# The last graph layer's dense products in 32-column tiles of TensorE, issued three rows at a time

## The chip, the cores and the metric

One Trainium2 chip, one of its cores. The metric is the device time of one execution in microseconds (us); runs are given by their median. The engines are TensorE (PE; its weight loads are listed apart as PEld), VectorE (DVE), ScalarE (ACT), GpSimd (POOL) and SyncE (SP), which here issues DMAs. All data of the changed part are fp32, but for the table of edge counts, which is bf16.

## The reference

A network of four layers on a graph of 3125 nodes with 256 features and 100,000 edges. Each layer adds a graph convolution and a mixer to x, then a feed-forward part with experts. The change is in the last layer's graph convolution, an attention over edges with four heads of 64 columns:

```python
xn = _layernorm(x)
x = x + _L3_gnn_ref(xn, edge_index, W, att_src, att_dst) + _L3_mix_ref(xn[None], ...)[0]
x = x + _L3_ffn_ref(_layernorm(x)[None], ...)[0]

def _gat_conv(x, edge_index, W, att_src, att_dst):
    xp = (x @ W).reshape(n, N_HEADS, HEAD_DIM)
    e = leaky_relu(a_src[src] + a_dst[dst], 0.2)
    e_exp = exp(e - segment_max(e, dst)[dst])
    alpha = e_exp / segment_sum(e_exp, dst)[dst]
    out = segment_sum(alpha[:, :, None] * xp[src], dst)
```

The mixer of this layer is a linear attention with a two-layer network behind it; the feed-forward part sends each node to one of eight experts.

## The kernel before, in words

Nodes lie in 25 blocks of 125 (`NB`, `P`); targets are also cut into pieces of 500 (`PIECES`, `PW`), the seventh of 125. The kernel computes this layer's sums over edges densely. For every source block, head and range of targets it forms a matrix z (source x target) of weights: the exponential of the leaky sum splits into factors of source and target, which ACT (L1965) and DVE (L1968) combine with the number of edges between each source and target, read from `ctt_d` into `cs`. The target factors lie in `rows`, a part of `xn`, loaded anew for each pair of pieces by `target_rows`. PE then multiplies z by the source block's features `xr` (L1971). `xr` has 65 columns per head: 64 features and a column of ones, whose product is the sum of the weights.

`l3_dense` takes the pieces two at a time, which gives three groups of 1000 targets and one of 125. For each group of 1000 it makes two passes of two heads each; the last group is one pass of four heads. A pass runs over the 25 source blocks (a row is one source block in one pass) and accumulates in four PSUM banks, one for each head and piece. So a row has two z of 125 x 1000 and four products of 65 x 500. At the end of a pass the banks are copied to SBUF (`evac`, turn by turn on DVE and ACT, L163 and L165), each block of 125 targets is turned on PE (L1987, in the last pass L1996), and `finish` (L1925 to L1932) divides by the sum, clips at zero and adds to `x`.

Next to `l3_dense` runs the mixer (`l3_mix_by_pieces`), a generator as it is; `together` (L1905) takes steps from the one that is behind, at a pace of 1.0 to 1.15. When both have delivered a piece (`arrive`), `follow` in `l3_ffn` normalizes it, turns it, finds its gate and expert (L2204 to L2255) and sends its rows to the experts by indirect DMAs on POOL; `l3_dense` hands its pieces over after row 5 of the next pass. After that the experts run. A scheduler that works at build time orders the instructions of each engine by their priorities, which go by the order in the program, and by its own estimates; each engine runs its list in order.

Of the kernel before, what the change touches and what calls it, by code (L numbers as in the profile page):

```python
# [12 lines left out]
F32 = mybir.dt.float32  # L13
# [4 lines left out]
AF = mybir.ActivationFunctionType  # L18
OP = mybir.AluOpType
# [4 lines left out]
N = 3125  # L24
D = 256
P = 125
NB = 25
# [10 lines left out]
PW = 500  # L38
# [52 lines left out]
def _tables():  # L91
# [12 lines left out]
    t[NT1 * 128:NT1 * 128 + NB, 0] = np.arange(NB) * P  # L104
    return np.ascontiguousarray(t.reshape(NT1 + 1, 128, 4).transpose(1, 2, 0))
EARLY = 0.25
PIECES = [(i, min(PW, N - i)) for i in range(0, N, PW)]


class Net:  # L110
    NE, TS = 16, 384

    def __init__(self, tc, a, ctx):
# [30 lines left out]
        self.col = col  # L144
        self.mean = c.tile([128, HB, len(PIECES)], F32, name="mean_p")

# [65 lines left out]
    def norm(self, src, dst):  # L212

        for i, w in PIECES:
            b0, b1 = i // P, (i + w) // P
            self.norm_rows(b1 - b0, src[:, b0:b1], dst[:, b0:b1])

    def expect(self, parts, follow=None, lag=0):

        self.waiting = {i: parts for i, _ in PIECES}  # L220
        self.follow = follow or self.norm_turn_piece
# [25 lines left out]
    def turn(self, src, dst):  # L247
        for i, w in PIECES:
            self.turn_piece(src, dst, i, w)
# [34 lines left out]

    def times_rows(self, pool, g, rows, e, out, add, pieces=PIECES):

# [107 lines left out]
    def counts(self, sb, wk, pt, px, py):  # L394
# [3 lines left out]
        self.cnt_d = self.dram.tile([NB, P, N], BF, name="cnt_d")  # L398
        self.ctt_d = self.dram.tile([len(PIECES), P, NB, PW], BF, name="ctt_d")
        i4 = sb.tile([128, 150, 4], BF, name="i4")  # L400
# [649 lines left out]
    def l0_ffn(self, fast=False):  # L1050
# [4 lines left out]
        with ExitStack() as s:  # L1055
# [69 lines left out]
            with ExitStack() as s2:  # L1125
                sums = None
                if fast:
# [3 lines left out]
                    with tc.issue_after(placed.ins):  # L1131
                        for part in sums:
                            if part > EARLY:
                                break
# [7 lines left out]
                for i in range(NT):  # L1142
# [29 lines left out]
                    for part in sums or ():  # L1172
                        if i + 1 < NT and part > EARLY + (1 - EARLY) * (i + 1) / NT:
                            break
# [662 lines left out]
    def l3_gnn_mix(self, before, arrivals):  # L1837
# [5 lines left out]
        nc, a = self.nc, self.a  # L1843
        with ExitStack() as s:
            ms = s.enter_context(self.pool("m3_sb"))
            with self.pool("m3_w") as sb:
                w = self.load_w(sb, "L3_gnn_W")
# [6 lines left out]
            sb = s.enter_context(self.pool("g3_sb"))  # L1854
            wk = s.enter_context(self.pool("g3_wk", 2))
            pa = s.enter_context(self.pool("g3_ps", 1, space=PSUM))
            xr = sb.tile([P, NB, 4, 65], F32, name="xr")
            nc.gpsimd.memset(xr[:, :, :, 64:65], 1.0)
            al = sb.tile([P, NB, 8], F32, name="al")
            for b in range(NB):  # L1860
                ps = self.bank()
                self.mm_tok(ps[:P, :264], self.xt, b, wx)
                nc.vector.tensor_copy(xr[:, b, :, :64], ps[:P, :D].rearrange("p (h d) -> p h d", h=4))
                nc.scalar.copy(al[:, b, :], ps[:P, 256:264])
            m = sb.tile([P, 8], F32, name="m")
            nc.vector.tensor_reduce(m, al.rearrange("p b h -> p h b"), axis=AX.X, op=OP.max)
            ps = self.bank()
# [5 lines left out]
            ps = self.bank()  # L1873
# [4 lines left out]
            bias = sb.tile([P, 4], F32, name="bias3")  # L1878
# [8 lines left out]
            r = sb.tile([P, 4, NB], F32, name="r3")  # L1887
            for h in range(4):
                nc.scalar.activation(r[:, h], al[:, :, 4 + h], AF.Exp, bias=bias[:, h:h + 1], scale=0.8)
            ps = self.bank()  # L1890
# [6 lines left out]
            us = sb.tile([P, 3, NB, 4], F32, name="us")  # L1897
# [16 lines left out]

    def l3_dense(self, sb, wk, pa, xr, us, r_d):

        nc = self.nc
        few = sb.tile([P, NB, 4], F32, name="few")
        free = self.xn.rearrange("p b d -> p (b d)")
        rows = free[:, :8 * PW].rearrange("p (h d) -> p h d", h=4)  # L1920
        at = free[:65, 8 * PW:12 * PW].rearrange("p (h d) -> p h d", h=2)

        def finish(b, h0, nh, acc):

            nc.vector.tensor_scalar(few[:, b, h0:h0 + nh], acc[:, :, 64], 1e-20, None, op0=OP.is_lt)  # L1925
            rd = wk.tile([P, 4], F32, name="rd")
            nc.vector.tensor_scalar(rd[:, :nh], acc[:, :, 64], 1e-20, None, op0=OP.max)
            nc.vector.reciprocal(rd[:, :nh], rd[:, :nh])
            t = wk.tile([P, 4, 64], F32, name="tf")
            nc.vector.tensor_mul(t[:, :nh], acc[:, :, :64], rd[:, :nh, None].to_broadcast([P, nh, 64]))  # L1930
            v = self.x[:, b, h0 * 64:(h0 + nh) * 64]
            nc.vector.scalar_tensor_tensor(v, t[:, :nh].rearrange("p h d -> p (h d)"), 0.0, v,  # L1932
                                           op0=OP.max, op1=OP.add)

        def target_rows(i, h0):

            n = min(2 * PW, N - i)
            for h in (h0, h0 + 1):
                if n > 0:
                    self.move(nc.sync, rows[:P, h, :n], r_d[h, i:i + n].partition_broadcast(P))  # L1940

        done, there = 0, []
        for h0 in (0, 2):
            target_rows(0, h0)
        for p0 in range(0, len(PIECES), 2):
            pcs = PIECES[p0:p0 + 2]
            n = sum(w for _, w in pcs)
            hg = 4 if n < PW else 2
            for h0 in range(0, 4, hg):
                acc = {}  # L1950
                for h in range(hg):
                    for k in range(len(pcs)):
                        acc[h, k] = pa.tile([65, 512], F32, name=f"acc{h * len(pcs) + k}")
                for b in range(NB):
                    cs = wk.tile([P, 2, PW], BF, name="cs", bufs=3)
                    if len(pcs) == 2:
                        self.move(nc.sync, cs, self.ctt_d[p0:p0 + 2, :, b, :].rearrange("k p d -> p k d"))
                        c = cs.rearrange("p k d -> p (k d)")
                    else:
                        self.move(nc.sync, cs[:, 0, :n], self.ctt_d[p0, :, b, :n])  # L1960
                        c = cs[:, 0, :n]
                    for h in range(hg):
                        k4 = h0 + h
                        t = wk.tile([P, 2 * PW], F32, name="t5")
                        nc.scalar.activation(t[:, :n], rows[:, k4, :n], AF.Relu, bias=us[:, 2, b, k4:k4 + 1],  # L1965
                                             scale=us[:, 0, b, k4:k4 + 1])
                        z = wk.tile([P, 2 * PW], F32, name="z", bufs=3)
                        nc.vector.scalar_tensor_tensor(z[:, :n], t[:, :n], us[:, 1, b, k4:k4 + 1], c,  # L1968
                                                       op0=OP.add, op1=OP.mult)
                        for k, (i, w) in enumerate(pcs):  # L1970
                            nc.tensor.matmul(acc[h, k][:, :w], xr[:, b, k4, :], z[:, k * PW:k * PW + w],  # L1971
                                             start=(b == 0), stop=(b == NB - 1))
                        done += n
                    yield done / (NB * N * 4)
                    if b == 5:
                        for i in there:
                            self.arrive(i)
                        there = []
                if hg == 2:
                    target_rows(pcs[0][0] + 2 * PW, h0)  # L1980
                    for h in range(2):
                        for k, (i, w) in enumerate(pcs):
                            self.evac(at[:, h, k * PW:k * PW + w], acc[h, k][:, :w])
                    for j in range(n // P):
                        ps = self.bank()
                        for h in range(2):
                            nc.tensor.transpose(ps[:P, h * 65:(h + 1) * 65], at[:, h, j * P:(j + 1) * P],  # L1987
                                                self.ident[:65, :65])
                        finish(p0 * 4 + j, h0, 2, ps[:P, :130].rearrange("p (h c) -> p h c", h=2))
                        yield done / (NB * N * 4)  # L1990
                else:
                    for h in range(4):
                        self.evac(at[:, h // 2, h % 2 * P:(h % 2 + 1) * P], acc[h, 0][:, :P])
                    ps = self.bank()
                    for h in range(4):
                        nc.tensor.transpose(ps[:P, h * 65:(h + 1) * 65], at[:, h // 2, h % 2 * P:(h % 2 + 1) * P],  # L1996
                                            self.ident[:65, :65])
                    finish(p0 * 4, 0, 4, ps[:P, :260].rearrange("p (h c) -> p h c", h=4))

            there = [i for i, w in pcs]  # L2000
        for i in there:
            self.arrive(i)
        nc.vector.tensor_reduce(self.viol[:P, 5:6], few.rearrange("p b h -> p (b h)"), axis=AX.X, op=OP.add)
# [421 lines left out]
```

## Time and profile before

| | us |
|---|---|
| median of 11 runs | 4812.44 (4802.48 to 4816.42) |
| the profiled execution | 4803.38 |
| its span | 4801.5 |
| PE busy in the span | 3740.6 |
| DVE busy | 2512.8 |
| ACT busy | 1303.2 |
| POOL busy | 1023.3 |
| mean clock granted to PE | 0.856 |

The profile is of one execution. A group's line gives line, engine, operation, output and inputs, shape and count; then busy time in us, the mean length of one in ns, and the engine's idle time ahead of it with what ended most of it. Lengths of PE's records contain a modelled end, so the distance between starts is the better measure of pace. An fp32 product shows as two records.

### The profile page before, as it was taken

How to read it: one execution, taken by the hardware profiler on the slowest of the kernel's cores; microseconds unless marked ns; L12 is line 12 of the kernel's file. 1: busy time of each engine (PE TensorE's matmuls, PEld its weight loads, DVE VectorE, ACT ScalarE, POOL GpSimd, SP SyncE). 2: the span in 40 equal slices, each digit the busy share in tenths (PEclk: the TensorE clock that was granted, in tenths of full speed). 3: DMA queues.
4: the chain of work that ended last, by engine and by line, in shares of the span. 5: the costliest groups of instructions: out<-in, count | busy, mean ns of one | idle time of the engine just before them, and what ended most of it. 6: DMA issues, size and time to landing. Idle time of an engine off the chain costs nothing. (4 is left out here: it accounts for less than half of the span.)

```text
span 4801.5 us, 50401 instructions
## 1 busy us (share of the span) xinstructions
PE 3740.6 (78%) x16695; PEld 2500.3 (52%) x16695; DVE 2512.8 (52%) x8604; ACT 1303.2 (27%) x2336; POOL 1023.3 (21%) x1041
## 2 busy tenths in 40 slices
PE   1887896599657899998454656666598999999698
PEld 0676795377534565555343445545365444444466
DVE  5877326544566319964222223333346677677544
ACT  1466100022123232233000000000145655556521
POOL 2000002300243000002666666666000000000011
PEclk8686896699878799999666777878799999999699
DMA  6244611344330000002333333333301222122232
GB/s 183 60 115 130 145 48 36 90 136 137 96 80 18 25 14 7 14 7 60 92 90 93 93 90 92 92 89 94 126 1 49 57 61 68 50 54 54 58 121 66
DMA packets 256035, 358.86 MB, mean 75 GB/s; under 512 B 62719, under 2 KB 199350, under 8 KB 255765
## 3 DMA queue, kind: packets, MB, share of 16 engines
q1 hardware_dynamic: 135900, 176.07, 12.5%
q0 software_dynamic: 62832, 126.93, 9.9%
q10 hardware_dynamic: 57033, 52.54, 3.9%
q8 instruction: 136, 2.23, 0.2%
q14 instruction: 134, 1.10, 0.1%
HBM read 268.73 MB, written 94.97 MB: 76 GB/s over the span
## 5 line engine op out<-in xcount | busy, mean ns | idle before, releaser
L1617 PE MATMUL acc<-hg,to 128*125 128x256 f32 x2042 | 597.7, 448 | 314.7 <-issue 160.6
L1601 POOL DMA_INDIRECT hg<-hx_d,idx x782 | 745.2, 953 | 414.9 <-issue 212.4
L1617 PEld LDWEIGHTS acc<-hg,to 128*125 128x125 f32 x2042 | 443.3, 224 | 447.5 <-issue 195.9
L1971 PE MATMUL acc<-z,xr 125*65 125x500 f32 (+1 forms) x1400 | 574.7, 553 | 15.0 <-DVE z L1968 13.5
L1612 DVE TENSOR_SCALAR to<-iota_w,rel_b,kw 128x125 f32<-128x125 f32 (+1 forms) x782 | 250.1, 376 | 428.2 <-remote 281.2
L1965 ACT ACTIVATE t<-xn,us 125x1000 f32<-125x1000 f32 (+1 forms) x400 | 409.4, 1037 | 237.5 <-DVE z L1968 226.0
L1968 DVE SCALAR_TENSOR_TENSOR z<-t,us,cs 125x1000 f32<-125x1000 f32 (+1 forms) x400 | 409.5, 1028 | 115.2 <-PE acc L1971 94.3
L1971 PEld LDWEIGHTS acc<-z,xr 125*65 125x65 f32 x1400 | 187.8, 144 | 314.6 <-issue 268.2
L261 PE MATMUL ps<-xt,w 128*128 128x500 f32 (+1 forms) x672 | 268.3, 546 | 1.6 <-DMA w<-in_L_ffn_W_dram 1.6
L1536 DVE SCALAR_TENSOR_TENSOR junk<-iota_w,rel_b,lock 128x125 f32<-128x125 f32 (+1 forms) x782 | 249.4, 401 | 0.0
L797 ACT ACTIVATE k<-k 125x128 f32<-125x128 f32 x50 | 15.8, 316 | 781.8 <-DVE k L796 495.6
L2255 POOL DMA_INDIRECT bx_d<-row,slot x25 | 31.2, 1249 | 886.5 <-ACT t L1965 420.9
L589 PE MATMUL ps<-y,cb 125*125 125x256 bf16 x1875 | 215.2, 280 | 0.0
L589 PEld LDWEIGHTS <-cb 125*125 125x125 bf16 x1875 | 214.0, 141 | 0.1
L190 ACT ACTIVATE rstd_t<-rstd_t 125x4 f32<-125x4 f32 (+2 forms) x86 | 17.2, 203 | 685.6 <-DVE rstd_t L189 561.2
L255 PE MATMUL ps<-wo,h 128*125 128x256 f32 x800 | 187.7, 386 | 3.6 <-ACT h L1439 2.6
L1445 DVE SCALAR_TENSOR_TENSOR x<-ps,lg,x 125x256 f32<-125x256 f32 x200 | 94.1, 489 | 173.5 <-PE ps L255 173.5
L261 PEld LDWEIGHTS ps<-xt,w 128*128 128x128 f32 x672 | 122.5, 193 | 114.0 <-issue 101.9
L261 PE MATMUL ps<-h,w 128*128 128x500 f32 (+1 forms) x448 | 179.5, 541 | 2.3 <-ACT h L1434 1.6
L255 PEld LDWEIGHTS ps<-wo,h 128*125 128x125 f32 x800 | 142.7, 187 | 66.0 <-ACT h L1439 43.7
L470 PE MATMUL t<-ky,lo 128*128 128x75 bf16 (+4 forms) x1251 | 138.9, 253 | 39.5 <-ACT ct L473 25.1
L243 PE MATMUL ps<-ident,xn 125*128 125x125 f32 x300 | 57.7, 342 | 139.9 <-DVE xn L209 128.9
(566 smaller groups left out, 6244.4 us busy)
## 6 DMA issues: line engine op xcount, KB each, us to landing
cs<-ctt_d SPq DMA_DIRECT2D x150, 218.8 KB
w<-in_L_ffn_w_dram SPq DMA_DIRECT2D x52, 512.0 KB
cnt_d<-cd SPq DMA_DIRECT2D x25, 683.6 KB
cb<-cnt_d SPq DMA_DIRECT2D x25, 683.6 KB
ctt_d<-ct ACTq DMA_DIRECT2D x6, 2734.4 KB
hg<-hx_d,idx POOLq DMA_INDIRECT x782
b0x_d<-zero SPq DMA_DIRECT2D x1, 9984.0 KB
xb<-b0x_d SPq DMA_DIRECT2D x26, 384.0 KB
```

Source lines behind the costliest of these rows:

```text
L255: self.nc.tensor.matmul(ps, xt[:, h, b * P:(b + 1) * P], w[:, h, :], start=(h == 0), stop=(h == k - 1))
L261: self.nc.tensor.matmul(ps, w[:, h, :], xt[:, h, i:i + n], start=(h == 0), stop=(h == k - 1))
L470: nc.tensor.matmul(t[:, w * 25 * r:(w + 1) * 25 * r], lo[:, :, n % 4], ky[:, :25 * r, n % 4], start=(j == 0), stop=(j == ws[w0 + w][2] - 1))
L589: nc.tensor.matmul(ps[:P, :D], cf[k][:, h * P:(h + 1) * P], y3[:, b0 + k, j, :], start=(k == 0 and j == 0), stop=(k == m - 1 and j == 2))
L1445: nc.vector.scalar_tensor_tensor(self.x[:, b, :], ps[:P, :D], g[:, b, e:e + 1], self.x[:, b, :], op0=OP.mult, op1=OP.add)
L1536: nc.vector.scalar_tensor_tensor(junk[:, :m * P], self.iota_w[:, :m * P], rel[:, c:c + 1], lock[:, b:b + m].rearrange("p b n -> p (b n)"), ...
L1601: nc.gpsimd.indirect_dma_start(out=hg[:, j, :], out_offset=None, in_=hx, in_offset=bass.IndirectOffsetOnAxis(ap=idx[:, c0 + j:c0 + j + 1], ...
L1612: nc.vector.tensor_scalar(to, self.iota_w[:, :nb * P], rel[:, c:c + 1], kw[:, j:j + 1], op0=OP.is_equal, op1=OP.mult)
L1617: nc.tensor.matmul(acc[k], to[:, (k - b) * P:(k - b + 1) * P], hg[:, j, :D], start=(c == first[k]), stop=(c == last[k]))
L1965: nc.scalar.activation(t[:, :n], rows[:, k4, :n], AF.Relu, bias=us[:, 2, b, k4:k4 + 1], scale=us[:, 0, b, k4:k4 + 1])
L1968: nc.vector.scalar_tensor_tensor(z[:, :n], t[:, :n], us[:, 1, b, k4:k4 + 1], c, op0=OP.add, op1=OP.mult)
L1971: nc.tensor.matmul(acc[h, k][:, :w], xr[:, b, k4, :], z[:, k * PW:k * PW + w], start=(b == 0), stop=(b == NB - 1))
```

## The change

`xr` loses its column of ones. A row's products are now 12 (four banks become three): for each piece, two heads by two halves of 32 columns fill the four 32-column tiles of one bank, and a third bank takes, for each piece and head, the product of z with 32 columns of ones, which gives the sum 32 times over. z has four buffers in place of three, and t moves to two spare pieces of `xn`. Dependencies without a semaphore chain all tile products of a row and its z's, so that they keep their order on PE; they are recorded at a higher priority (600). Every third row (`BURST`) the last product that isn't one of them is noted, and the burst that begins three bursts later (`LAG`) stands behind it. A pass's banks are three out of four in turn. At the end of a pass all targets of a piece are turned by whole transposes of 128 columns, and the division is done for a piece at a time.

The order of the built program on PE, from the first to the last of these products: before, 700 products of L1971 and 731 others, in 313 stretches; after, 2100 tile products and 700 others, in 153 stretches.

```diff
+BURST, LAG = 3, 3
...
-            xr = sb.tile([P, NB, 4, 65], F32, name="xr")
-            nc.gpsimd.memset(xr[:, :, :, 64:65], 1.0)
+            xr = sb.tile([P, NB, 4, 64], F32, name="xr")
...
+        spare = [free[:P, j * PW:(j + 2) * PW] for j in (8, 10)]
+        groups = [PIECES[p:p + 2] for p in range(0, len(PIECES), 2)]
...
+        def finish(b, nb, h0, nh, acc):
+
+            w, nu = nb * P, len(acc) - 1
+            at = wk.tile([128, 3, PW], F32, name="at", bufs=1)
+            for k in range(nu + 1):
+                self.evac(at[:, k, :w], acc[k][:, :w])
+            ps = self.bank()
+            for j in range(nb):
+                nc.tensor.transpose(ps[:P, j * 128:(j + 1) * 128], at[:, nu, j * P:(j + 1) * P], self.ident)
+            sums = ps[:P, :nb * 128].rearrange("p (j q r) -> p j q r", j=nb, r=32)[:, :, :, 0]
...
+            for k in range(nu):
...
+                for j in range(nb):
+                    nc.tensor.transpose(ps[:P, j * 128:(j + 1) * 128], at[:, k, j * P:(j + 1) * P], self.ident)
+                t = wk.tile([P, 4, 2, 64], F32, name="tf")
+                nc.vector.tensor_mul(t[:, :nb], ps[:P, :nb * 128].rearrange("p (j h d) -> p j h d", j=nb, d=64),
+                                     rd[:, :nb, 2 * k:2 * k + 2, None].to_broadcast([P, nb, 2, 64]))
...
+                units = [(h0, k, w) for h0 in hs for k, (_, w) in enumerate(pcs)]
+                acc = [pa.tile([128, 512], F32, name=f"acc{(turn + j) % 4}") for j in range(3)]
+                turn += 3
...
-                        t = wk.tile([P, 2 * PW], F32, name="t5")
+                        t = spare[h % 2]
...
-                        z = wk.tile([P, 2 * PW], F32, name="z", bufs=3)
+                        z = zs[h] = wk.tile([P, 2 * PW], F32, name="z", bufs=4)
...
-                            nc.tensor.matmul(acc[h, k][:, :w], xr[:, b, k4, :], z[:, k * PW:k * PW + w],
-                                             start=(b == 0), stop=(b == NB - 1))
+                    if steps % BURST == 0:
+                        marks.append(next((i for i in reversed(nc.cur_bb.bb.instructions)
+                                           if i.engine == mybir.EngineType.PE and i.name not in own), None))
+                        if len(marks) > LAG and marks[-1 - LAG] is not None:
+                            made.append(marks[-1 - LAG])
+                    steps += 1
+                    with self.tc.high_priority(600):
+                        for out, left, h0, j, k, w, q in (
+                                [(acc[u], xr[:, b, h0 + j, f:f + 32], h0, j, k, w, 64 * j + f)
+                                 for u, (h0, k, w) in enumerate(units) for j in range(2) for f in (0, 32)]
+                                + [(acc[2], self.ones[:P, :32], h0, j, k, w, 64 * u + 32 * j)
+                                   for u, (h0, k, w) in enumerate(units) for j in range(2)]):
+                            mm = nc.tensor.matmul(out[q:q + 32, :w], left, zs[h0 + j][:, k * PW:k * PW + w],
+                                                  start=(b == 0), stop=(b == NB - 1), tile_position=(0, q))
+                            for i in made:
+                                self.tc.add_manual_dep(mm.ins, i.name, row, reason="in one row")
+                            made = [mm.ins]
+                            own.add(mm.ins.name)
```

More of the change, by code (lines that the diff above doesn't have):

```diff
@@ L1862, in l3_gnn_mix @@
                 self.mm_tok(ps[:P, :264], self.xt, b, wx)
-                nc.vector.tensor_copy(xr[:, b, :, :64], ps[:P, :D].rearrange("p (h d) -> p h d", h=4))
+                nc.vector.tensor_copy(xr[:, b], ps[:P, :D].rearrange("p (h d) -> p h d", h=4))
                 nc.scalar.copy(al[:, b, :], ps[:P, 256:264])
@@ L1920, in l3_dense @@
         rows = free[:, :8 * PW].rearrange("p (h d) -> p h d", h=4)
[L1921 to L1939, printed above, removed]
-                    self.move(nc.sync, rows[:P, h, :n], r_d[h, i:i + n].partition_broadcast(P))
-        done, there = 0, []
+        spare = [free[:P, j * PW:(j + 2) * PW] for j in (8, 10)]
+        groups = [PIECES[p:p + 2] for p in range(0, len(PIECES), 2)]
+        def target_rows(g, h0):
+            if g < len(groups):
+                i, n = groups[g][0][0], sum(w for _, w in groups[g])
+                for h in (h0, h0 + 1):
+                    self.move(nc.sync, rows[:P, h, :n], r_d[h, i:i + n].partition_broadcast(P))
@@ new lines, in finish @@
+        def finish(b, nb, h0, nh, acc):
[7 more added lines that the diff above has]
+            sums = ps[:P, :nb * 128].rearrange("p (j q r) -> p j q r", j=nb, r=32)[:, :, :, 0]
+            rd = wk.tile([P, 4, 4], F32, name="rd")
+            f = wk.tile([P, 4, 4], F32, name="fw")
+            nc.vector.tensor_scalar(f[:, :nb], sums, 1e-20, None, op0=OP.is_lt)
+            nc.vector.tensor_scalar(rd[:, :nb], sums, 1e-20, None, op0=OP.max)
+            nc.vector.reciprocal(rd[:, :nb], rd[:, :nb])
+            for k in range(nu):
+                bk, hk = (b + 4 * k, h0) if nh == 2 else (b, 2 * k)
+                nc.vector.tensor_copy(few[:, bk:bk + nb, hk:hk + 2], f[:, :nb, 2 * k:2 * k + 2])
+                ps = self.bank()
+                for j in range(nb):
[3 more added lines that the diff above has]
+                                     rd[:, :nb, 2 * k:2 * k + 2, None].to_broadcast([P, nb, 2, 64]))
+                v = self.x[:, bk:bk + nb, hk * 64:hk * 64 + 128]
+                nc.vector.scalar_tensor_tensor(v, t[:, :nb].rearrange("p j h d -> p j (h d)"), 0.0, v,
+                                               op0=OP.max, op1=OP.add)
@@ L1943, in l3_dense @@
+        done, there, turn, made, marks, steps, own = 0, [], 0, [], [], 0, set()
+        row = mybir.DependencyInfo(mybir.DependencyClass.NoSync, mybir.DependencyReason.DATA)
         for h0 in (0, 2):
             target_rows(0, h0)
-        for p0 in range(0, len(PIECES), 2):
-            pcs = PIECES[p0:p0 + 2]
+        for g, pcs in enumerate(groups):
+            b0 = pcs[0][0] // P
             n = sum(w for _, w in pcs)
[L1948 to L1953, printed above, removed]
+            for hs in ((0, 2),) if len(pcs) == 1 else ((0,), (2,)):
+                units = [(h0, k, w) for h0 in hs for k, (_, w) in enumerate(pcs)]
+                acc = [pa.tile([128, 512], F32, name=f"acc{(turn + j) % 4}") for j in range(3)]
+                turn += 3
@@ L1956, in l3_dense @@
                     if len(pcs) == 2:
-                        self.move(nc.sync, cs, self.ctt_d[p0:p0 + 2, :, b, :].rearrange("k p d -> p k d"))
+                        self.move(nc.sync, cs, self.ctt_d[2 * g:2 * g + 2, :, b, :].rearrange("k p d -> p k d"))
                         c = cs.rearrange("p k d -> p (k d)")
                     else:
-                        self.move(nc.sync, cs[:, 0, :n], self.ctt_d[p0, :, b, :n])
+                        self.move(nc.sync, cs[:, 0, :n], self.ctt_d[2 * g, :, b, :n])
@@ L1961, in l3_dense @@
                         c = cs[:, 0, :n]
-                    for h in range(hg):
-                        k4 = h0 + h
-                        t = wk.tile([P, 2 * PW], F32, name="t5")
-                        nc.scalar.activation(t[:, :n], rows[:, k4, :n], AF.Relu, bias=us[:, 2, b, k4:k4 + 1],
-                                             scale=us[:, 0, b, k4:k4 + 1])
-                        z = wk.tile([P, 2 * PW], F32, name="z", bufs=3)
[L1968 to L1971, printed above, removed]
-                                             start=(b == 0), stop=(b == NB - 1))
-                        done += n
+                    zs, made = {}, made[-1:]
@@ new lines, in l3_dense @@
+                    for h in [h0 + j for h0 in hs for j in range(2)]:
+                        t = spare[h % 2]
+                        nc.scalar.activation(t[:, :n], rows[:P, h, :n], AF.Relu, bias=us[:, 2, b, h:h + 1],
+                                             scale=us[:, 0, b, h:h + 1])
+                        z = zs[h] = wk.tile([P, 2 * PW], F32, name="z", bufs=4)
+                        made.append(nc.vector.scalar_tensor_tensor(z[:, :n], t[:, :n], us[:, 1, b, h:h + 1], c,
+                                                                   op0=OP.add, op1=OP.mult).ins)
@@ L1974, in l3_dense @@
+                    done += n * 2 * len(hs)
                     yield done / (NB * N * 4)
@@ L1978, in l3_dense @@
                         there = []
[L1979 to L1998, printed above, removed]
+                for h0 in hs:
+                    target_rows(g + 1, h0)
+                finish(b0, pcs[0][1] // P, hs[0], 2 * len(hs), acc)
+                yield done / (NB * N * 4)
             there = [i for i, w in pcs]
```

## The prediction

> **What bounds the kernel now.** I read the page first (busy shares, the 40 slices, the costliest groups), then the window of the changed lines by engine, then the waits inside it, then the order of TensorE's products there. The last graph layer's products are line L1971; its first and last starts bound a window from 3672 to 4532 us, 860 of the span's 4801.5 us.
>
> ```profile
> L1971 PE MATMUL acc<-z,xr 125*65 125x500 f32 (+1 forms) x1400 | 574.7, 553 | 15.0 <-DVE z L1968 13.5
> L1965 ACT ACTIVATE t<-xn,us 125x1000 f32<-125x1000 f32 (+1 forms) x400 | 409.4, 1037 | 237.5 <-DVE z L1968 226.0
> L1968 DVE SCALAR_TENSOR_TENSOR z<-t,us,cs 125x1000 f32<-125x1000 f32 (+1 forms) x400 | 409.5, 1028 | 115.2 <-PE acc L1971 94.3
> ```
> ```profile
> 3672.00:4532.00 860.00, 828.75 (x2620) 379.88 (x2618) 598.51 (x1293) 512.72 (x627) 30.04 (x24) 0.97 0.20 54
> 4444.00:4532.00 88.00, 69.27 (x303) 43.65 (x301) 59.48 (x245) 58.39 (x121) 9.55 (x8) 0.73 0.11 25
> ```
>
> The second fence is the busy time by engine of the window and of its last 88 us: PE, weight loads, DVE, ACT, POOL, then the granted clock. PE is busy 829 of 860 us; DVE 599, ACT 513. DVE sits idle 94 us in front of L1968 because PE has not yet released a z; PE waited for a z only 13.5 us. So PE bounds the window, and 575 of its 829 us are L1971. The other 254 us are the mixer and the routing, which run in between. Only the last 88 us are different: there a row has four heads of 125 targets, ACT needs 4 x 0.49 us a row, PE is busy 69 of 88 us.
>
> The products in between are long chains across engines, and today they cost PE no idle time. The timeline of PE inside one of the mixer's attention steps:
>
> ```profile
> 4319.49 1.84 PE L1971 MATMUL acc<-z,xr 125*65 125x500 f32 x4
> 4321.17 0.27 PE L1340 MATMUL ps<-ident,o 125*128 125x125 f32 x1
> 4321.28 2.68 PE L1971 MATMUL acc<-z,xr 125*65 125x500 f32 x6
> 4323.79 0.48 PE L1340 MATMUL ps<-ident,o 125*128 125x125 f32 x3
> 4324.11 3.52 PE L1971 MATMUL acc<-z,xr 125*65 125x500 f32 x8
> 4327.46 0.38 PE L1340 MATMUL ps<-ident,o 125*128 125x125 f32 x2
> ```
>
> Columns: start, length, line, number of records. Each L1340 transpose waits for four DVE steps on its block, and L1971 fills every wait. This also gives the pace: from 4321.28, six records later, to 4323.79, and from 4324.11, eight records later, to 4327.46, 0.419 us each. One fp32 product of 500 columns is two such records (1400 records for 700 products), 0.838 us.
>
> **The change, part by part.**
>
> *The products.* A row (one source block, two heads, 1000 targets) has 4 products of 65 columns now: 4 x 0.838 = 3.35 us. After, it has 12 products of 32 columns, in three rounds over the four column tiles. If the four tiles of a round stream side by side, a round costs one product's time: 3 x 0.838 = 2.51 us. The saving is 0.84 us a row, over 6 passes x 25 rows = 150 rows **-126 us**. In the last 25 rows PE isn't the bound (ACT's 1.96 us a row is), so I count nothing there. If tiles do not run side by side at all, a row costs 24 x 0.419 = 10.06 us. No two products run side by side in this trace, so this is the disputed price; bounds -126 and +1006 us. I take -126: the four tiles write disjoint partitions, and nothing in the rows above shows a resource that one 32-column product would need whole.
>
> *Changing the mode.* The built program has the tile products in 77 stretches on PE with 76 stretches of others between, so 152 changes between whole and tiled array. The trace has such changes elsewhere. L291 is a product with 16 output columns, in a 32-column tile; L1076 before it uses the whole array. L297 uses 32 rows, L1321 after it the whole:
>
> ```profile
> 799.32 1.54 PE L1076 MATMUL ps<-both,ones 125*128 125x400 f32 x2
> 800.65 1.04 PE L291 MATMUL ps<-ident,g 125*16 125x125 f32 x4
> ```
> ```profile
> 1537.32 1.48 PE L297 MATMUL ps<-bo,gt 8*125 8x256 f32 x3
> 1538.73 1.68 PE L1321 MATMUL ps<-bd,q_e 128*125 128x132 f32 x6
> ```
>
> The clock granted in both stretches was 0.50. 400 fp32 columns took 0.667 us each at it: 799.32 + 2 x 0.667 = 800.65, no time lost. Coming back, 3 x 0.427 us lead to 1538.60 and L1321 starts at 1538.73: 0.13 us, and its second record is a further 0.16 us late. So a change costs 0 to 0.29 us; I take 0.13 us: 152 x 0.13 = **+20 us** (0 to 44). The Trainium skill says of this ("TensorEngine Tiling (Array Packing)", Key Properties) that changing the tiling mode drains TensorE. The rows agree only coming back, with those 0.13 us.
>
> *The cover.* The tile products stand in stretches of mostly 36 (three rows, 7.5 us), and what was threaded between them stands together: the eight attention products, eight transposes and eight products behind them of one piece are one stretch of 24, and so are the routing's transposes, gates and counts (19 to 45). Inside a stretch nothing covers the chain any more. Attention: per block DVE needs 0.16 (L1325) + 0.20 (L1326) + 2 x 0.28 (L1328) = 0.92 us, 3.7 us for four blocks, then an ACT copy of about 0.5 us; PE's own work there that can overlap is about 1.2 us: 3 us idle, 7 pieces, 21 us. Routing: from gate to counts softmax, four max/find pairs (0.155 + 0.08 + 0.16 us each) and a table load of 1.28 us, together 4.8 us, 6 times, 29 us. And DVE works off such a chain in runs of 30 to 60 operations (18 us for 60 at 0.3 us) ahead of the next z; four z buffers hold two rows, 5 us of PE's work, so the third row of the next burst is some 3 us late, 6 times, 18 us. Sum **+70 us**; between 0 (all hidden) and double, 140 us.
>
> *z, t, buffers.* L1965 and L1968 keep count and shape. Per row DVE needs 2 x 1.255 and ACT 2 x 1.22 us, against 2.51 us on PE: just enough. z has four buffers in place of three.
>
> *The end of a pass.* DVE did 48 times five small steps (L1925 to L1932: 6.9 + 7.1 + 7.6 + 13.9 + 13.9 = 49 us); now 7 times three small ones and, per 500 columns, a copy and two steps of 512 elements, some 22 us by the 1.22 us of a 1024-element step. DVE wins 27 us, not on the path (599 of 860 us). Some 75 whole transposes (0.16 us each by L1340) replace 99 of L1987 and L1996 (15.5 us): nothing. The fourth accumulator bank is free when a pass begins, the second is needed 0.84 us later and its copy takes 0.57 to 0.67 us: nothing. The queues of SP and POOL keep their transfers (a memset less on POOL).
>
> Sum: 4803.4 (the profiled execution) - 126 + 20 + 70 = **4767 us**. The median of the runs is 9 us above that execution, so **4776 us**. By itself this case reaches from 4686 (no cover lost, no cost of changes) to 4870 us.
>
> **Rivals.**
> 1. *The two records of a product stand in each other's way: slower.* An fp32 product is issued as load, matmul, load, matmul on one tile, before the next tile's. All L1971 starts are in order and 0.419 us apart. If a start must wait for the one before it in the queue, the second record of tile 1 waits for the first, and tile 2's first waits with it: only two records ever overlap, and a product costs 0.419 us. Row: 12 x 0.419 = 5.03 us against 3.35, 150 x 1.68 = +252, with the changes +20: 5075 us, as a median 5084. It decides from 8 products' time a row upwards. For it: in the trace the order is kept without exception. Against it: no row here has two tiles, so none shows that order is kept across them.
>    The Trainium skill ("TensorE: Matmul & The Clock Gate", Part 3) speaks for this rival: matmuls start and end strictly in program order, only weight loads are pulled ahead. By that rule alone the sum would be this rival's.
> 2. *The cover costs more than the tiles bring.* If in each of some 50 bursts DVE makes the first row's two z only after the chain, 2.5 us a burst, 125 us are lost: 4803 - 126 + 20 + 125 = 4822, as a median 4831. It decides from 106 us of lost cover, 2.1 us a burst. Against it: in most bursts two rows of z can be ready.
> 3. *Tiles run one after another*: +1006 us, about 5830. No row excludes it.
>
> **Chances.** Forecast's case 0.62 (0.56 faster by over 0.2%, 0.06 within; 0.2% is about what a measurement of this kernel can tell from no change); rival 1 0.18; rival 2 0.16 (0.03 within 0.2%, 0.13 slower); rival 3 0.04. Faster 0.56, same 0.09, slower 0.35. Range 4690 to 5085 us, since leaving out rivals 1 and 3 alone would leave out more than 2 in 10; the likeliest case's own is 4690 to 4870.
>
> **What would show it.** Starts of tile products: four within a few ns and 0.838 us a round (mine), or steps of 0.419 us (rival 1). The window of the layer some 825 us long. PE's idle time in it grows from 31 us to about 100, named by DVE's attention and routing lines and by z. A gap at a change over 0.3 us, a granted clock well under 0.97 in the window, or DVE over 90% busy would prove the sum wrong.

## The result, and the profile after

The changed kernel takes 4823.53 us (median of 14 runs, 4816.76 to 4836.13), the kernel before 4808.63 us (53 runs): ratio 1.0033, 95% interval [1.0024, 1.0043]. It is 0.33% slower; I had forecast 4776 us.

The page of the changed kernel, the groups of the changed lines:

```profile
L1986 DVE SCALAR_TENSOR_TENSOR z<-xn,us,cs 125x1000 f32<-125x1000 f32 (+1 forms) x400 | 400.3, 1027 | 135.6 <-PE acc L2002 72.0
L1983 ACT ACTIVATE xn<-xn,us 125x1000 f32<-125x1000 f32 (+1 forms) x400 | 405.8, 1038 | 186.8 <-DVE z L1986 178.1
L2002 PE MATMUL acc<-z,xr 125*32 125x500 f32 (+1 forms) x2800 | 380.5, 562 | 20.2 <-DVE z L1986 16.8
...
L2002 PE MATMUL acc<-z,ones 125*32 125x500 f32 (+1 forms) x1400 | 223.7, 551 | 0.0
```

And its window from the first to the last of these products, with the last 88 us:

```profile
3676.00:4554.00 878.00, 782.49 (x5386) 350.49 (x5385) 577.20 (x1101) 505.38 (x620) 30.48 (x24) 0.91 0.20 54
4466.00:4554.00 88.00, 71.46 (x738) 39.46 (x731) 54.31 (x212) 54.12 (x117) 9.61 (x8) 0.71 0.12 25
```

The window is 878 us long, 18 more than before. PE is busy 46 us less, not 126; its idle time is 96 us in place of 31, and its granted clock 0.91 in place of 0.97.

The tiles themselves do what was hoped. The timeline of PE at three rows of one burst, with x16 and x8 records a row:

```profile
4104.56 1.88 PE L2002 MATMUL acc<-z,xr 125*32 125x500 f32 x16
4106.26 1.02 PE L2002 MATMUL acc<-z,ones 125*32 125x500 f32 x8
4107.10 1.86 PE L2002 MATMUL acc<-z,xr 125*32 125x500 f32 x16
4108.77 1.02 PE L2002 MATMUL acc<-z,ones 125*32 125x500 f32 x8
4109.61 2.14 PE L2002 MATMUL acc<-z,xr 125*32 125x500 f32 x16
4111.29 1.31 PE L2002 MATMUL acc<-z,ones 125*32 125x500 f32 x8
```

From row to row it is 2.54 and 2.51 us, against 3.35 before. In the records of a round (from 3680.805 us) the four tiles start at .805, .812, .818 and .825, their second records 0.44 us later, and the next round's first ones 0.42 us after those.

**Where the time went.** I took the records of PE from the layer's first product to its last, and called each stretch of the layer's products "own" and each stretch between "others". A record streams its columns at 0.833 ns each at full clock (500 columns 0.417 us, as in the trace's pace of 0.419), a tile's a quarter of that for each of four. What half clock adds is "slow clock"; what is left of a stretch, up to the next one's start, is "rest": waits, changes of mode, rounds with less than four tiles.

| us | region | own: streaming | own: slow clock | own: rest | others: streaming | others: slow clock | others: rest | at half clock |
|---|---|---|---|---|---|---|---|---|
| before | 858.5 | 520.8 | 13.1 | 38.9 | 245.6 | 4.4 | 35.8 | 54.6 |
| after | 875.7 | 390.6 | 15.7 | 81.9 | 245.0 | 20.1 | 122.5 | 153.6 |

So -131 us of streaming, and against it +87 us of rest between the bursts, +43 inside them, and +18 of slow clock: +17 us in all. The largest term is the chains that nothing covers now. One attention step in the changed kernel, PE's timeline:

```profile
3854.61 1.24 PE L2002 MATMUL acc<-z,ones 125*32 125x500 f32 x8
3855.78 2.06 PE L1322 MATMUL ps<-bd,q_e 128*125 128x132 f32 x16
3859.34 0.30 PE L1341 MATMUL ps<-ident,o 125*128 125x125 f32 x1 [1.50 <-DVE o L1329]
3860.09 1.71 PE L1341 MATMUL ps<-ident,o 125*128 125x125 f32 x5 [0.45 <-DVE o L1329]
3862.16 0.68 PE L1341 MATMUL ps<-ident,o 125*128 125x125 f32 x2 [0.35 <-DVE o L1329]
3863.29 4.89 PE L256 MATMUL ps<-L_mix_Wm,ot 128*125 128x256 f32 x13 [0.46 <-ACT ot L1342]
```

All sixteen records of the eight products go first, and then each transpose waits for DVE in the open. Before, layer products lay between those transposes. The routing is worse; PE's timeline there, then the step of DVE that PE's last line waits for, and a step of ACT that stands behind the same transfer:

```profile
4280.50 0.60 PE L2251 MATMUL ps<-hot,before 125*125 125x32 f32 x2 [5.63 <-DVE hot L2247]
4280.91 0.61 PE L2252 MATMUL ps<-hot,ones 125*125 125x32 f32 x2
4291.97 0.68 PE L2230 MATMUL ps<-ident,row 125*128 125x125 f32 x2 [10.45 <-DVE row L210]
```
```profile
4291.51 1.38 DVE L210 TENSOR_SCALAR row<-x,ln_mv,ln_rs 125x256 f32<-125x256 f32 x4 [8.06 <-DMA bx_d<-row,slot]
```
```profile
4291.48 1.05 ACT L2223 COPY row<-x 125x1024 f32<-125x1024 f32 x1 [13.30 <-DMA bx_d<-row,slot]
```

PE waits 5.63 us for the gate's chain on DVE, and soon after 10.45 us for `row`, whose buffer is free only when a piece's transfer to the experts has landed; from 4280 to 4292 us it works 1.05 us. PE's six largest waits in the window of the changed kernel, by line (total, times, longest):

```profile
PE ps L2230 <- DVE row L210: 22.3, 4, 10.5
PE acc L2002 <- DVE z L1986: 16.8, 29, 3.1
PE ps L2251 <- DVE hot L2247: 15.3, 4, 5.6
PE ps L1341 <- DVE o L1329: 9.6, 12, 1.5
PE ps L2064 <- ACT ot L2057: 8.9, 1, 8.9
PE ps L2055 <- DVE o L2092: 5.5, 1, 5.5
```

In the kernel before, the two largest in front of others' products were:

```profile
PE ps L2211 <- DVE row L209: 5.6, 2, 2.9
PE ps L2232 <- DVE hot L2228: 2.7, 1, 2.7
```

All waits of PE in front of others' products sum to 75 us after and to 16 before. Two of the waits for `row` are of 10 us. The one that ends at 4292 us is behind the transfer; the one that ends at 4031.6 us is not: there DVE works off the mixer's last steps on the piece (L2092, L2069 to L2072) and then its layer norm, from 4022 us on without a pause. The 8.9 us at L2064 (up to 3990.9 us) are behind a transfer again: DVE waited 9.7 us for it (L2272, up to 3986.3 us), ACT 9.9 us for a z of DVE, and PE for ACT.

### The profile page after: what moved, and what is told of

Same layout as the page of the kernel before. It is cut to its first block, busy times and chain, and to the rows that moved or that the text cites. A ratio compares the mean times of both kernels' runs of the same rounds, so it can differ in the third digit from the quotient of the medians.

```text
span 4821.8 us, 55688 instructions
## 1 busy us (share of the span) xinstructions
PE 3687.6 (76%) x19470; PEld 2464.7 (51%) x19470; DVE 2496.5 (52%) x8419; ACT 1297.6 (27%) x2332; POOL 1027.1 (21%) x1040
## 5 line engine op out<-in xcount | busy, mean ns | idle before, releaser
L1986 DVE SCALAR_TENSOR_TENSOR z<-xn,us,cs 125x1000 f32<-125x1000 f32 (+1 forms) x400 | 400.3, 1027 | 135.6 <-PE acc L2002 72.0
L1983 ACT ACTIVATE xn<-xn,us 125x1000 f32<-125x1000 f32 (+1 forms) x400 | 405.8, 1038 | 186.8 <-DVE z L1986 178.1
L2002 PE MATMUL acc<-z,xr 125*32 125x500 f32 (+1 forms) x2800 | 380.5, 562 | 20.2 <-DVE z L1986 16.8
L798 ACT ACTIVATE k<-k 125x128 f32<-125x128 f32 x50 | 15.7, 315 | 783.7 <-DVE k L797 332.8
L2002 PE MATMUL acc<-z,ones 125*32 125x500 f32 (+1 forms) x1400 | 223.7, 551 | 0.0
L2002 PEld LDWEIGHTS acc<-z,xr 125*32 125x32 f32 x2800 | 104.2, 113 | 220.6 <-issue 132.6
```

The costliest lines, as they stand in the source:

```text
L1983: nc.scalar.activation(t[:, :n], rows[:P, h, :n], AF.Relu, bias=us[:, 2, b, h:h + 1], scale=us[:, 0, b, h:h + 1])
L1986: made.append(nc.vector.scalar_tensor_tensor(z[:, :n], t[:, :n], us[:, 1, b, h:h + 1], c, op0=OP.add, op1=OP.mult).ins)
L2002: mm = nc.tensor.matmul(out[q:q + 32, :w], left, zs[h0 + j][:, k * PW:k * PW + w], start=(b == 0), stop=(b == NB - 1), tile_position=(0, q))
```

## The experiments

All numbers of one group come from one chip, beside runs of the kernel before there: 4809.04 us on the first, 4666.65 on the second (its stages ahead of this layer are some 140 us shorter), 4799.40 on the third. So ratios and differences are compared, and between profiled executions the length of the layer's region rather than the span, since the region's start moves by up to 24 us even on one chip.

| | us | ratio to before [95%] | region | own: rest | others: rest | at half clock |
|---|---|---|---|---|---|---|
| whole3 | 4894.44 | 1.0179 [1.0162, 1.0196] | 944.0 | 28.2 | 108.6 | 153.6 |
| noprio | 4791.21 | 0.9972 [0.9958, 0.9987] | 834.1 | 133.9 | 50.6 | 61.4 |
| z6 | 4785.01 | 0.9942 [0.9926, 0.9959] | 829.9 | 52.6 | 111.1 | 133.1 |
| row1 | 4841.47 | 1.0052 [1.0034, 1.0070] | 883.0 | 80.1 | 127.9 | 170.7 |
| atom_z6 (chip 2) | 4578.86 | 0.9811 [0.9794, 0.9827] | 766.0 | 68.2 | 45.2 | 53.3 |
| atom (chip 2) | 4605.79 | 0.9874 [0.9858, 0.9891] | 798.9 | 96.5 | 52.3 | 58.0 |
| noprio_z6 (chip 2) | 4619.27 | 0.9905 [0.9888, 0.9921] | 808.6 | 107.9 | 49.8 | 61.4 |
| whole_z5 (chip 2) | 4646.04 | 0.9959 [0.9944, 0.9973] | 844.8 | 32.2 | 30.0 | 47.4 |
| after_again (chip 3) | 4816.44 | 1.0035 [1.0022, 1.0048] | 872.0 | 83.0 | 122.0 | 136.5 |
| due_only (chip 3) | 4787.22 | 0.9974 [0.9963, 0.9986] | 841.8 | 133.7 | 55.0 | 75.1 |
| prio_only (chip 3) | 4879.09 | 1.0164 [1.0138, 1.0190] | 925.2 | 158.4 | 100.7 | 110.6 |
| atom_z6_again (chip 3) | 4712.59 | 0.9816 [0.9796, 0.9835] | 764.2 | 68.6 | 44.6 | 51.2 |

My theory: the tiles gain their 126 us, and standing in bursts costs more cover (work of PE that lies over a chain's waits) than that. The rival: the tiles gain less (changes of mode, z too late), and the bursts are not to blame.

**whole3**: the order of the change without its tiles. The products are those of before (65 columns, whole array), with the bursts of three rows, the due times (the dependencies that put a burst behind other products noted three bursts before), the priority and four z.

```diff
-                            nc.tensor.matmul(acc[h, k][:, :w], xr[:, b, k4, :], z[:, k * PW:k * PW + w],
+                    with self.tc.high_priority(600):
...
+                                mm = nc.tensor.matmul(acc[h, k][:, :w], xr[:, b, h0 + h, :],
+                                                      zs[h][:, k * PW:k * PW + w],
```

> The products stay whole (65 columns, four a row), but stand in bursts of three rows, at the priority and with the due times of the change, z in four buffers. Theory (lost cover: grouping exposes the mixer's and the routing's chains): the other products' stretches lose some 85 us and the slower clock some 18 us more than before, with no tile gain against it: 4870 to 4915 us. Rival (the tiles' own costs, that is changes of mode, tiles out of step, eat the gain): grouping is cheap, 4800 to 4825 us.

Measured +85.4 us. Its region by engine, and PE's longest waits there:

```profile
3675.60:4619.60 944.00, 861.82 (x2607) 403.46 (x2606) 605.88 (x1290) 512.52 (x623) 30.10 (x24) 0.92 0.19 49
```
```profile
PE ps L2227 <- DVE row L210: 26.9, 4, 10.5
PE ps L2248 <- DVE hot L2244: 15.4, 5, 3.3
```

These products use no 32-column tile, so there is no change to one, yet the same lines wait (their numbers are 3 lower here), these two as long as in the changed kernel or longer, and the clock is 0.92. The built order is by the same rules but not the same: 107 stretches in place of 153. Against before the others' rest grew by 73 us and slow clock by 26, while the layer's own rest shrank by 11. From here to the changed kernel the region gains 68: -130 of streaming, +54 of own rest, +14 of others' rest, and the remainder clock. So the new order costs 85 us, and two fifths of what the tiles gain goes inside the layer's own stretches.

**noprio**: the tiles without the priority and without due times.

```diff
-                            made.append(marks[-1 - LAG])
+                            pass
...
-                    with self.tc.high_priority(600):
+                    if True:
```

> Tiles as in the change, but without the higher priority and the due times: the scheduler threads them between the other products again (265 stretches on PE in place of 153). Theory (lost cover): cover comes back for the price of 112 more changes of mode at 0.095 us, 11 us: 4740 to 4790 us. Rival (tiles' own costs): more changes, more rounds broken, 4830 to 4860 us.

Measured -17.8 us, 1 us outside the theory's range. The rest between falls from 122 to 51 us, as the theory wants, but the rest inside rises from 82 to 134: a row is cut into 16 records here and there (the median length of an own stretch; 48 in the changed kernel), and a round of two tiles takes as long as one of four.

**z6**: the changed order, with z made in place of t, in six buffers.

```diff
-                        t = spare[h % 2]
+                        zi = zn % 6
+                        zn += 1
+                        t = zs[h] = (spare[zi // 3] if zi % 3 == 0 else
+                                     wk.tile([P, 2 * PW], F32, name="z", bufs=4))
...
-                        z = zs[h] = wk.tile([P, 2 * PW], F32, name="z", bufs=4)
-                        made.append(nc.vector.scalar_tensor_tensor(z[:, :n], t[:, :n], us[:, 1, b, h:h + 1], c,
+                        made.append(nc.vector.scalar_tensor_tensor(t[:, :n], t[:, :n], us[:, 1, b, h:h + 1], c,
```

> The change with z made in place in t and six buffers for it (three rows in place of two and a separate t). Theory (lost cover, of which a part is the z that comes late to the third row of a burst; the tile stretches lose 43 us more than the whole products' did): 20 to 40 us less than the change, 4785 to 4805 us. Rival (tiles out of step and mode changes make up the loss within the stretches): within 8 us of the change, 4815 to 4830 us.

Measured -24.0 us. In the first rows the changed kernel's rows begin 2.55 and 2.73 us apart by turns; here each is 2.51 us after the last. Own rest is 29 us less. So z was not just in time: where only one of a row's z is ready, two tiles start alone. The first row of the changed kernel shows it: two tiles at 3677.412 and .418, the other two at 3678.126 and .132, and the two pairs stay out of step until the burst ends with two tiles alone. In a burst of three whole rows at full clock this costs 0.2 to 0.35 us (7.90 to 8.03 us in the changed kernel, 7.68 here). z6's built order also cuts fewer rows (58 stretches of the layer's products in place of 77), so the 29 us are of both and not of late z alone.

**row1**: bursts of one row, due nine bursts later, to put the others between single rows.

```diff
-BURST, LAG = 3, 3
+BURST, LAG = 1, 9
```

> The change with bursts of one row, due nine bursts later (the same nine rows): 227 stretches on PE in place of 153. Theory (lost cover): a part of the cover comes back, 4780 to 4810 us. Rival (tiles' own costs): 74 more changes of mode and no gain from cover, 4825 to 4845 us.

Measured +32.4 us: a miss, and where the rival stood. The median stretch of layer products is 24 records in place of 48, but the same chains wait in the open:

```profile
PE ps L2230 <- DVE row L210: 22.9, 4, 10.4
PE ps L2251 <- DVE hot L2247: 14.8, 4, 5.1
```

So the length of a burst is not what loses the cover. I changed the theory: the priority does, which the runs of the third chip test below. It puts a row on PE as soon as its z are there, so that no row is left to lie under a chain when one comes.

**atom_z6, atom, noprio_z6**: three versions with no due times. In the first two only a row's first product has the normal priority, and the eleven that follow it the high one: a row is placed when its turn comes, but then it is not cut. atom_z6 and noprio_z6 have z6's buffers as well. Beside the two edits of noprio, the first two have:

```diff
+                            with ExitStack() as up:
+                                if out is not acc[0] or q:
+                                    up.enter_context(self.tc.high_priority(600))
+                                mm = nc.tensor.matmul(out[q:q + 32, :w], left, zs[h0 + j][:, k * PW:k * PW + w],
```

> Six z buffers made in place, no due times, and of a row's twelve products only the first at normal priority: rows stay whole, and the other products come back between single rows (211 stretches on PE). Theory (lost cover, late z, and rounds broken by threading): all three are mended, 4725 to 4765 us. Rival (late z alone is the loss, grouping costs nothing): as with six buffers in groups of three rows, 4775 to 4795 us.

> The same threading of whole rows (217 stretches), with the change's four z buffers and separate t. Theory: the other products' cover is back and rounds are whole, late z remains: 4745 to 4780 us. Rival (late z alone): as the change, 4815 to 4833 us.

> Six z buffers in place with the free threading of the run without priorities, which cuts rows at 9 and 3 products (271 stretches). Theory: z no longer late, but rounds of four tiles are broken by the cuts: 4765 to 4790 us, behind the version with whole rows by 15 us or more. Rival (late z alone): 4755 us or less, level with the version with whole rows.

The times in these texts are for a chip like the first; read as differences, the versions gave -87.8, -60.9 and -47.4 us. atom lies within the theory's range, the other two 3 to 4 us beyond theirs, on the faster side; the rivals are refuted. All keep the rest between at 45 to 52 us and the half clock below 62 us. Uncut rows take 37 to 40 us of own rest away (noprio 133.9 to atom 96.5, noprio_z6 107.9 to atom_z6 68.2), six z some 27. Own stretches have 24 records in the median in atom as in row1, and both have four z, so these two differ in priority and due times, not in the size of a burst.

**whole_z5**: the kernel before, with z in place and five buffers.

```diff
-                        t = wk.tile([P, 2 * PW], F32, name="t5")
+                        t = wk.tile([P, 2 * PW], F32, name="z", bufs=5)
...
-                        z = wk.tile([P, 2 * PW], F32, name="z", bufs=3)
+                        z = t
```

> The kernel before with z made in place and five buffers for it in place of three and two for t; products whole. Theory: with whole products PE sets the pace and waits for a z only 13.5 us in all, so nothing to gain: 4798 to 4815 us. Rival (the buffers are worth as much by themselves as they were in tiles, 38 us): 4770 to 4785 us.

Measured -20.6 us, between the two ranges (as differences, theory -11 to +6, rival -39 to -24): z was a small limit before the change too. Its region is 14 us shorter than that of the kernel before. Of atom_z6's 88 us some 20 can thus be had without a tile; 67 us (4646.04 to 4578.86) are the tiles' and their order's.

**The two parts of the order apart**, on a third chip, with the changed kernel and the best version beside them.

```diff
 prio_only: -                            made.append(marks[-1 - LAG])
            +                            pass
 due_only:  -                    with self.tc.high_priority(600):
            +                    if True:
```

> The changed kernel without the high priority of the layer's products; the due times of three rows stay. In the built order the layer's products then stand in 269 stretches, as in the version without both. Theory (the high priority makes the clumps, the due times alone do not): -10 to -30 us against before, as the version without both (-18). Rival (the due times make the clumps): +5 to +25 us, as the changed kernel.

> The changed kernel with the high priority and without the due times. In the built order nothing calls the mixer's and the router's products until the layer's have run out, so more of them stand together and behind. Theory (chains that run with no layer product between their links cost the time): +20 to +100 us against before, worse than the changed kernel. Rival (it is the due times that cut into the layer's rows): below the changed kernel, -20 to +5 us.

> The changed kernel once more, so that the other three runs of this call have it on their own chip. It was 0.33% behind the kernel before; I expect +8 to +24 us (ratio 1.002 to 1.005). If the loss belongs to one chip's state and not to the order of the work, it would come out within 0.1% or ahead.

> The version with only a row's first product at normal priority, no due times and six buffers of z, once more, beside the changed kernel on one chip. Theory (lost cover is what the change pays, the tiles themselves gain): -75 to -100 us against the kernel before, so some 90 to 115 us ahead of the changed kernel. Rival (the first result came from a chip on which the earlier stages are faster): -20 to -50 us.

| ratio to before | normal priority | priority 600 |
|---|---|---|
| without due times | 0.9972 (noprio) | 1.0164 (prio_only) |
| with due times | 0.9974 (due_only) | 1.0035 (after_again) |

noprio's ratio is from the first chip, the other three are from the third.

Their regions by engine, due_only, then prio_only, then atom_z6_again:

```profile
3672.50:4514.30 841.80, 791.31 (x5381) 331.97 (x5380) 571.05 (x1100) 500.67 (x614) 30.05 (x24) 0.96 0.21 56
```
```profile
3670.80:4596.00 925.20, 852.05 (x5377) 341.80 (x5376) 572.66 (x1074) 506.35 (x616) 25.16 (x20) 0.94 0.19 51
```
```profile
3667.30:4431.50 764.20, 731.19 (x5381) 319.22 (x5382) 557.95 (x1100) 488.17 (x617) 31.92 (x24) 0.97 0.23 62
```

The priority costs 0.6% with the due times and 1.9% without; due times mend two thirds of it, and without the priority they change nothing. In prio_only the layer runs ahead: 784 of its 4200 records lie in the first tenth of the region (480 in due_only), only 92 in the ninth, where 195 of the others are left. The theory's number held; its reason only in part, as that kernel loses even more inside its cut rows (158 us) than between them (101).

The best version comes out at 0.9816 [0.9796, 0.9835] again, 86.8 us ahead of the kernel before and 104 ahead of the changed one on one chip. PE's waits in its region, all but the shorter ones:

```profile
PE acc L2007 <- DVE z L1988: 14.0, 19, 3.9
PE ps L2235 <- DVE row L210: 6.6, 2, 3.3
```

`row` still comes late, but PE waits 6.6 us for it in place of 22.3; the gate's chain (`hot`) isn't waited for at all. For the z that lie in `xn`'s spare pieces PE waits a further 4.7 us.

## Why the prediction was wrong, point by point

- **What bounds the kernel**: right in the main. PE bounds the window, and a row's pace set what it could gain, though whole_z5 finds some 20 us that z's buffers cost before. The last pass, where I counted nothing, went from 75.3 to 80.5 us (first to last product of 125 columns).
- **The products, -126**: right; the layer's streaming fell by 130, since the last 25 rows have 5 us less of it too (where it gains nothing).
- **The order of records on PE (rivals 1 and 3)**: refuted by starts 6 to 7 ns apart. The Trainium skill ("TensorE: Matmul & The Clock Gate", Part 3) says that matmuls start and end strictly in program order. If a product's two records are issued one behind the other, as rival 1 has it, the measured starts do not keep that order: its second record starts 0.44 us after its first, behind the first records of three other tiles. The profile does not show the order of issue.
- **Changing the mode, +20**: near. At full clock a change costs 0.095 us each way (median of 133 changes in the changed kernel, deciles 0.094 to 0.096; 0.003 between such stretches before), some 14.5 us for 152. It is in the rest above. The pairs of rows that I had read showed nothing going in and 0.13 us coming back, at half clock, and no row shows that L291 and L297 stand in 32-wide tiles. The Trainium skill says that a change of tiling mode drains TensorE ("TensorEngine Tiling (Array Packing)", Key Properties); 0.095 us lost each way agrees with that.
- **z, t, buffers, "just enough"**: wrong. z6 shows up to 29 us for it, rows that are cut less often included. My "the third row is some 3 us late, 6 times, 18 us" had the right place but not the consequence: where one of a row's z is late, two tiles start alone, and the pairs stay out of step.
- **The end of a pass, nothing**: not tested by itself. DVE's busy time in the window fell by 21 us, of which 9 are L1986's (27 forecast).
- **The cover, +70**: this is the step that failed. The mechanism is right and the term too small. Region by region it was -131 (products) + 14.5 (mode) + 133.5 = +17, so the cover with everything behind it cost 133.5 us where I had put 70, with 140 as its upper bound.
  - In the sum: attention 13 us (21 forecast; PE's waits for `o`, `q_e` and `ot` rose by that), routing 32 (29 forecast), the layer's own rest without its changes of mode 36 (18 forecast for the late z; cut rows are in it).
  - Not in the sum at all: the mixer's last step (L2055, L2064) 14 us, the slow clock 18, and 20 of the others' rest that no wait names.
  - The routing was near by luck. Most of it is the two waits of 10 us for `row`, which are not in the forecast's reasons: one stands behind the mixer's last steps on DVE, one behind a transfer. The trace of before shows the transfers as waits of DVE (L2253, 25.9 us in all, 4 times); PE was busy through the two longest, of 12.5 and 7.9 us.
  - One reading of the built order was wrong: 24 of the 77 stretches have 36 products, and the median has 24, so "mostly 36" was too many.
- **Rival 2**, at 0.16, foresaw the outcome: it decides from 106 us of lost cover. It put the loss in z made behind the chains. That is 36 us of the 133.5 at most; PE's named waits for the chains rose by 59.
- **What would show it**: PE's idle time of "about 100" was hit by luck (96 us), as the window was 878, not 825 us. The granted clock, 0.91 in place of 0.97, gave one of the signs that I had named. Busy time hid the rest: it counts a round of two tiles, a record at half clock and a modelled end as work.

What stays open: what the 20 us of the others' added rest are that neither a wait (59 of 87) nor the changes of mode (7) name; why the priority without due times cuts so many rows; and whether the priority of DVE's z steps could mend the changed order, which was not tried.

## What to carry to other kernels

A group of products saves two changes of mode, at most 0.2 us here, and what stood between them had been the cover of chains through DVE, ACT and a transfer, worth several us each: price what a group uncovers before what it saves. Work that can fill any gap did better here without a priority above the chains'; what helped was only enough of it to keep a unit (a row of twelve products) whole. And read a tiled product's gain from starts and streaming, not from PE's busy time.

## What the runs showed of the hardware

Four 32-column tiles stream fp32 products fully side by side: rounds of 0.84 us for four products of 500 columns, each product in two records of 0.42 us. Going from the whole array to these tiles, or back, loses 0.095 us at full clock.

The clock falls without a long pause. Ahead of the half-clock stretch that begins at 3860.2 us in the changed kernel, PE's two windows of 3.4 us read:

```profile
3853.40:3856.80 3.40, 3.40 (x33) 1.91 (x26) 3.16 (x3) 3.18 (x3) 0.00 (x0) 1.00 0.32 78
3856.80:3860.20 3.40, 1.45 (x12) 1.10 (x10) 3.16 (x10) 2.60 (x3) 0.00 (x0) 0.99 1.03 275
```

PE was busy 43% of the second; its longest pause there was 1.50 us, and the clock was half for the next 6.8 us. Of the 13 falls of the clock in this region, one came after 3.4 us without any work on PE; in the 3.4 us ahead of eight others the longest pause was 0.8 to 2.0 us. In the layer's region of all these traces half-clock stretches last 3.4 to 51.2 us, each a multiple of 3.41 us. Versions that leave chains uncovered spend 111 to 171 us of the region at half clock, the others 47 to 75.
